# Seven block products in place of eight for two pairs of row tiles, with the weight differences on GpSimd

## The chip, the cores and the metric

The kernel runs on one core of a Trainium2 chip. The metric is the device time of one execution in microseconds. The median of three runs of the kernel before is 498.72 us (497.08 to 500.88).

## What is computed

Two layers in a row, over x of 2 x 1024 rows by 2048 columns. The first normalizes x, quantizes it and a context matrix to 8 bits, multiplies them and adds the product, times a gate, to x. The second normalizes the result, quantizes each row by its own largest value, multiplies by a weight that is rounded to -1, 0 or 1, and adds that product, times a gate, to its input. Cut to what matters:

```python
def _L0_xattn_ref(x1, x2, x1_scale, x1_zp, x2_scale, x2_zp):
    q1 = fake_quant(x1, x1_scale, x1_zp)      # clip(round(x / s + z), 0, 255), then (q - z) * s
    q2 = fake_quant(x2, x2_scale, x2_zp)
    return jnp.matmul(q1, q2)

def _L0_ffn_ref(x, weight):
    s = QP / jnp.clip(jnp.max(jnp.abs(x), axis=-1, keepdims=True), 1e-05, None)
    xq = jnp.clip(jnp.round(x * s), QN, QP) / s
    scale_w = 1.0 / jnp.clip(jnp.mean(jnp.abs(weight)), EPS, None)
    tw = jnp.clip(jnp.round(weight * scale_w), -1.0, 1.0)
    return jnp.einsum('bsi,oi->bso', xq, tw) / scale_w

x = x + jnp.tanh(g_xattn[0]) * _L0_xattn_ref(_layernorm(x), ctx_4096, ...)
x = x + jnp.tanh(g_ffn[0]) * _L0_ffn_ref(_layernorm(x), L0_ffn_weight)
```

x is (2, 1024, 2048), the context (2, 2048, 2048), the weight (2048, 2048).

## The kernel before

**Tiles.** Rows are cut into 16 tiles of 128: tiles 0 to 7 are the first batch, 8 to 15 the second. A tile of x (f32, 128 x 2048) stays in SBUF as `resid` from its load to its store. The second batch goes through in the order `rows` = 14, 15, 8, 9, 10, 11, 12, 13. In the code's key names these are x,6, x,7, x,0 to x,5, since a tile of the second batch lies where one of the first was.

**Stages of a tile.** `norm1` (statistics, L378; quantization on ScalarE, ACT, L434; clip on VectorE, DVE, L437), then a transpose by DMA into one of five `turned` buffers. `first(t, h)` multiplies it with half h of the context (1024 columns) in eight steps of four matmuls (L611) and adds the result to `resid` on DVE (L620). `column_term` sums the context's columns with PE (L581, evicted by DVE, L586), and `terms` adds these sums to a tile (L640: two SBUF tensors in, 128 x 2048). `norm2` takes the mean (L668), squares on ACT (L677), the largest square on DVE (L684), then for a group of two tiles together: `var` (L690 to L693), a square root on ACT (L697), `scale` with `newton` (L360, L366 to L368, L703, L704) and `product_scale` (L708, L709). `norm2_tile` quantizes on ACT (L748), casts on DVE (L757) and transposes by DMA (L774). `second(t, h)` multiplies with half h of the ternary weight: two units of 16 matmuls (L814), one for each quarter of 512 output columns; then an add on DVE (L823) and a store (L829), issued by GpSimd (POOL), and for the last two tiles by SyncE (SP).

**Memory.** `ca` holds the quantized context of the running batch, in 16 slots ("ca", 0) to ("ca", 15), eight for each half of the columns; slot p of half h is read by step p of every `first(t, h)`. `tw` holds the weight as fp8. PSUM has three buffers `mm` of 128 x 1024 f32, that `first` and `second` take in turn and the adds on DVE give back, and two small ones `tr`.

**The order of the work** is not left to the engines. Every piece is a step of a `Plan` with an engine, a length, a due time and what it reads and writes. `order` lays the steps out by due time as their inputs and buffers come free; `latest` works backwards from the end for new due times; ten rounds of this are made and the best order is given out. So each engine has one fixed list and takes it in order. Steps with `port=True` are planned so that DVE and POOL do not run them at once; on the chip nothing but their data holds them apart.

Of the kernel before, what the change touches and what calls it, by code (L numbers as in the profile page):

```python
# [9 lines left out]
F32 = mybir.dt.float32  # L10
# [13 lines left out]
class Plan:  # L24
# [128 lines left out]
    def give_out(self):  # L153
        steps = self.steps
        waits = [len(s[4]) for s in steps]
        follow = [[] for _ in steps]
        for n, s in enumerate(steps):
            for m in s[4]:
                follow[m].append(n)
        due, best = [s[2] for s in steps], None  # L160
        for i in range(self.ROUNDS):
            order, ends, passed = self.order(due, follow, waits)
            if best is None or max(ends) < best[0]:
                best = (max(ends), order)
            due = self.latest(ends, passed, follow)
        for n, slot in best[1]:
            if slot is None:
                steps[n][3]()
            else:
                steps[n][3](slot)  # L170
# [3 lines left out]
def flamingo_gated_kernel(  # L174
# [117 lines left out]
    plan = Plan({"work": NWORK, "tp": NTP, "mm": 3, "tr": 2})  # L292
    step = plan.step
    aT, qT, pm = {}, {}, {}
    taken = {}

    def scalars():

        s = {}

        def spread(slot):
            s["pp"] = tr[slot]
            nc.tensor.matmul(s["pp"][:, 2:6], ones32[0:1, :], par1[:, 2:6], start=True, stop=True)
            nc.tensor.matmul(s["pp"][:, 0:2], ones32[0:1, :], tg1, start=True, stop=True)

        def of(i, rs, zc):
            nc.vector.reciprocal(rs, par[:, i : i + 1])  # L310
            nc.vector.tensor_scalar(zc, par[:, i + 1 : i + 2], CENTER, None, ALU.subtract)

        def rest():
            nc.vector.scalar_tensor_tensor(g1, par[:, 2:3], par[:, 4:5], tg[:, 0:1], ALU.mult, ALU.mult)
            nc.vector.scalar_tensor_tensor(g1d1, zc1, -1.0, g1, ALU.mult, ALU.mult)
            nc.vector.scalar_tensor_tensor(g1d2, zc2, -1.0, g1, ALU.mult, ALU.mult)
            nc.vector.tensor_scalar(kd2, zc2, -float(K), None, ALU.mult)
            nc.vector.tensor_scalar(gkd, kd2, g1d1, None, ALU.mult)

        step("ACT", 0.3, 0.0, lambda: nc.scalar.activation(tg1, par1[:, 0:2], AF.Tanh), wr=[("tg1",)], hold=4.0)  # L320
        by = step("PE", 0.6, 6.0, spread, rd=[("tg1",)], wr=[("pp",)], take="tr", hold=6.8)
        step(
            "DVE", 0.2, 6.0, lambda: nc.vector.tensor_copy(par, s["pp"][:, 0:6]), rd=[("pp",)],
            wr=[("par",)], give=[by],
        )
        step("DVE", 0.3, 6.1, lambda: of(2, rs1, zc1), rd=[("par",)], wr=[("p1",)])
        step("DVE", 0.3, 6.2, lambda: of(4, rs2, zc2), rd=[("par",)], wr=[("p2",)])
        step("DVE", 0.9, 10.0, rest, rd=[("p1",), ("p2",)], wr=[("g",)])

    def res(t):  # L330
        return resid[:, t % MT, :]

    def xk(t, h=None):
        return [("x", t % MT, i) for i in ((0, 1) if h is None else (h,))]

    strip = const.tile([P, 30 * 2 * MT], F32, name="strip")
    stats6 = const.tile([P, 4, K // 512, nc.vector.BN_STATS_DIM], F32, name="stats6")
    used = [0]

    def tiny(n=1):  # L340
        used[0] += n
        return strip[:, used[0] - n : used[0]]


    def load_x(t, due, queue, halves=1, hold=0.0):
        w = K // halves
        for h in range(halves):

            def bring(h=h):
                q = nc.sync if queue == "SP" else nc.gpsimd  # L350
                q.dma_start(out=res(t)[:, ts(h, w)], in_=xrow[t][:, ts(h, w)])

            keys = xk(t) if halves == 1 else xk(t, h)
            step(queue, 0.5, due, bring, wr=keys, dma=2.55 / halves, hold=hold)

    def newton(v, sd):

        n = v.shape[1]
        r, f = tiny(n), tiny(n)
        nc.vector.reciprocal(r, sd)  # L360
        if n == 1:
            nc.vector.tensor_scalar(f, v, r, r, ALU.mult, ALU.mult)
            nc.vector.tensor_scalar(f, f, -0.5, 1.5, ALU.mult, ALU.add)
            nc.vector.tensor_scalar(r, r, f, None, ALU.mult)
        else:
            nc.vector.scalar_tensor_tensor(f, r, -0.5, r, ALU.mult, ALU.mult)  # L366
            nc.vector.tensor_mul(f, f, v)
            nc.vector.scalar_tensor_tensor(r, f, 1.5, r, ALU.add, ALU.mult)  # L368
        return r

    def norm1(group, dues, by_pe, fold_it, place=None, pieces=1, on_dve=False):

        n = len(group)
        s = {"mv": tiny(2 * n)}
        key = lambda *a: ("n1", group[0]) + a

        def stats(t, c):
            nc.vector.bn_stats(stats6[:, t % 4, c, :], res(t)[:, ts(c, 512)])  # L378

        def aggr(j, t):  # L380
            nc.vector.bn_aggr(s["mv"][:, ts(j, 2)], stats6[:, t % 4].rearrange("p c s -> p (c s)"))

        def root():
            s["sd"] = tiny(n)
            nc.scalar.activation(s["sd"], s["ve"], AF.Sqrt)

        def var():
            mv = s["mv"].rearrange("p (n s) -> p s n", s=2)
            s["mean"], s["ve"] = mv[:, 0, :], tiny(n)
            nc.vector.tensor_scalar(s["ve"], mv[:, 1, :], LN_EPS, None, ALU.add)  # L390

        def scale():
            r = newton(s["ve"], s["sd"])
            sc, bi = s["sc"], s["bi"] = tiny(n), tiny(n)
            nc.vector.tensor_scalar(sc, r, rs1, None, ALU.mult)
            if n == 1:
                nc.vector.tensor_scalar(bi, s["mean"], sc, -1.0, ALU.mult, ALU.mult)
            else:
                nc.vector.scalar_tensor_tensor(bi, s["mean"], -1.0, sc, ALU.mult, ALU.mult)
            nc.vector.tensor_scalar(bi, bi, zc1, None, ALU.add)  # L400

        for j, t in enumerate(group):
            for c in range(4):
                step(
                    "DVE", 0.69, dues[j], (lambda t, c: lambda: stats(t, c))(t, c), rd=xk(t, c // 2),
                    wr=[("st", t % 4)],
                )
            step(
                "DVE", 0.3, dues[j], (lambda j, t: lambda: aggr(j, t))(j, t), rd=[("st", t % 4)],
                wr=[key("mv")],  # L410
            )
        due = dues[-1]
        step("DVE", 0.16, due, var, rd=[key("mv")], wr=[key("ve")])
        step("ACT", 0.2, due, root, rd=[key("ve")], wr=[key("sd")])
# [4 lines left out]

    def norm1_tile(t, due, by_pe, fold_it, place, pieces, ready, scales, on_dve):  # L420

        s = {}
        key = lambda *a: ("n1t", t) + a
        n = K // pieces

# [699 lines left out]
```

## Time and profile before

| what | value |
|---|---|
| median of three runs | 498.72 us |
| the profiled execution: its time | 496.74 us |
| the profiled execution: its span | 495.0 us |
| `first`, L611, matmuls in the trace, spaced 0.216 us | 1024 |
| `second`, L814, 512-column matmuls in the trace | 976 |
| POOL's 24 TENSOR_TENSOR of 128x512 f16 (L460, L462) | 1.15 to 2.13 us each, 15 to 88 us |
| DVE L557, two SBUF tensors, 128x2048 f16, before 90 us | 1.22 to 2.17 us |
| the same after 240 us | 1.22 us |
| DVE L640, two SBUF tensors, 128x2048 f32 | 2.34 us |
| DVE L823, one PSUM and one SBUF tensor, 128x1024 f32 | 1.28 us |
| granted PE clock over the span | 0.995 |

The span is cut into stages by what PE does: up to 170 us it waits at times for data, context and weight (the two layers of the first batch meet there); from 170 us to the end it works without a gap. From 342 to 373 us PE runs `first` of the second batch, from 373 to 428 `second` of the second batch with a last tile's `first` among it, from 428 to 491 `second` alone. A line of the timeline gives start and length in us, engine, line, operation, out<-in, shape and count, and in brackets the engine's idle time before it and what ended that. A matmul's own length (379 ns) is longer than its distance to the next one (216 ns), since they are pipelined.

### The profile page before, as it was taken

The page shows a single profiled execution, that of the slowest core. Times are in us where ns is not written, and L with a number is a line of the kernel's source. Part 1 is how long each engine was busy: PE and PEld are TensorE (multiplying, and loading weights), DVE is VectorE, ACT ScalarE, POOL GpSimd, SP SyncE. Part 2 cuts the span into 40 slices and gives each one's busy share as a digit, 9 for nine tenths or more (in the row PEclk, how much of TensorE's full clock was granted, in tenths as well). Part 3 has the DMA queues.
Part 4 walks back from the last instruction along what each step waited for, and adds up shares of the span by engine and source line. Part 5 has one row for each costly group of instructions (what it writes and reads, how often), then busy time and mean ns, then how long its engine had stood idle before and what let it go on. Part 6 is the DMA issues. An engine that isn't in the chain of part 4 may idle for free.

```text
span 495.0 us, 6179 instructions
## 1 busy us (share of the span) xinstructions
PE 467.6 (94%) x2422; PEld 223.0 (45%) x2422; DVE 340.6 (69%) x568; ACT 276.6 (56%) x258; POOL 63.5 (13%) x76
## 2 busy tenths in 40 slices
PE   0599999999998799999999999999999999999996
PEld 0244454444467344444444444444444444444442
DVE  4999989959999688556697957632989831572122
ACT  4997896878999988631488364530454430050000
POOL 0574529100000020100100100000000000000000
PEclk9999999999999899999999999999999999999999
DMA  8999968992189999999999995610041542215122
GB/s 293 425 419 424 366 214 338 428 407 81 60 215 366 260 301 295 306 258 330 402 363 341 297 269 189 100 28 1 0 66 47 144 111 102 86 61 153 79 92 85
DMA packets 76170, 108.94 MB, mean 220 GB/s; under 512 B 58220, under 2 KB 58220, under 8 KB 70892
## 3 DMA queue, kind: packets, MB, share of 16 engines
q1 hardware_dynamic: 72064, 93.86, 60.1%
q0 software_dynamic: 4064, 14.68, 7.7%
q8 instruction: 19, 0.31, 0.2%
q14 instruction: 11, 0.09, 0.1%
q10 hardware_dynamic: 12, 0.00, 0.0%
HBM read 77.59 MB, written 16.78 MB: 191 GB/s over the span
## 4 chain that ended last, share of the span: by engine, by line
PE 76%; DVE 14%; DMA 6%; issue 2%; ACT 1%; DVEq 0%
PE mm L814 40%; PE mm L611 32%; DVE resid L640 3%; DMA resid<-in_x_dram 2%; PE tr L814 2%; DVE strip L684 2%; DMA tw<-in_ctx_dram 2%; DVE resid L620 2%; DMA tw<-ca 2%; DVE stats L378 1%; DVE ca L550 1%; DVE ca L903 1%; ACT ca L547 1%; PE tr L444 1%; DVE colg L557 1%
## 5 line engine op out<-in xcount | busy, mean ns | idle before, releaser
L814 PE MATMUL mm<-tw,turned 128*128 128x512 fp8e4 (+1 forms) x1104 | 211.9, 353 | 4.7 <-DMA turned<-work 2.4
L611 PE MATMUL mm<-ca,turned 128*128 128x512 f16 x832 | 187.7, 384 | 0.5 <-DVE ca L550 0.3
L814 PEld LDWEIGHTS <-turned 128*128 128x128 f16 x1168 | 106.8, 98 | 122.7 <-issue 6.3
L611 PEld LDWEIGHTS <-turned 128*128 128x128 f16 x832 | 81.8, 99 | 99.0 <-issue 4.8
L823 DVE SCALAR_TENSOR_TENSOR resid<-mm,am,resid 128x1024 f32<-128x1024 f32 (+1 forms) x31 | 38.6, 1246 | 64.3 <-PE mm L814 64.2
L547 ACT ACTIVATE ca<-ca,scal 128x2048 int16<-128x2048 f32 (+1 forms) x30 | 50.5, 1692 | 36.9 <-DMA ca<-in_ctx_dram 36.4
L677 ACT ACTIVATE work<-resid,strip 128x1024 f32<-128x1024 f32 x32 | 36.4, 1138 | 57.8 <-DVE strip L668 54.1
L829 POOL DMA_DIRECT2D out_dram<-resid x30 | 18.1, 606 | 362.5 <-DVE resid L823 225.2
L620 DVE SCALAR_TENSOR_TENSOR resid<-mm,scal,resid 128x1024 f32<-128x1024 f32 x32 | 40.4, 1277 | 18.4 <-PE mm L611 18.2
L378 DVE BATCH_NORM_STATS2 stats<-resid 128x6 f32<-128x512 f32 x64 | 40.0, 678 | 7.9 <-DMA resid<-in_x_dram 7.9
L550 DVE TENSOR_SCALAR ca<-ca 128x2048 f16<-128x2048 int16 (+1 forms) x40 | 27.3, 698 | 24.5 <-ACT ca L547 24.5
L611 PE MATMUL mm<-ca,tw 128*128 128x512 f16 x192 | 43.1, 379 | 0.4 <-DVE tw L450 0.2
L748 ACT ACTIVATE work<-resid,strip 128x2048 int16<-128x2048 f32 x16 | 35.5, 2263 | 12.2 <-DVE strip L704 7.8
L684 DVE TENSOR_REDUCE strip<-work 128x1 f32<-128x1024 f32 x32 | 37.3, 1210 | 1.3 <-ACT work L677 1.3
L640 DVE SCALAR_TENSOR_TENSOR resid<-colg,rowg,resid 128x2048 f32<-128x2048 f32 x16 | 37.4, 2344 | 0.1
L434 ACT ACTIVATE work<-resid,strip 128x2048 int16<-128x2048 f32 (+1 forms) x17 | 33.4, 1984 | 1.3 <-DVE strip L400 1.3
L557 DVE TENSOR_TENSOR colg<-colg,ca 128x2048 f16<-128x2048 f16 x24 | 30.8, 1304 | 0.3
L611 PEld LDWEIGHTS <-tw 128*128 128x128 f16 x192 | 18.4, 98 | 22.8 <-DVE tw L450 0.7
L899 ACT ACTIVATE work<-ca,scal 128x2048 int16<-128x2048 f32 x13 | 25.6, 2005 | 1.6 <-DMA ca<-in_L_ffn_weight_dram 1.1
L473 ACT ACTIVATE work<-work,scal 128x2048 f16<-128x2048 f16 x8 | 16.0, 1994 | 18.5 <-DMA turned<-work 18.5
L865 ACT ACTIVATE tw<-ca 128x2048 int8<-128x2048 f32 x10 | 19.1, 1910 | 7.6 <-DMA ca<-in_L_ffn_weight_dram 7.5
L462 POOL TENSOR_TENSOR tw<-tw,work 128x512 f16<-128x512 f16 x16 | 21.8, 1364 | 1.6 <-DVE work L437 0.4
(93 smaller groups left out, 260.7 us busy)
## 6 DMA issues: line engine op xcount, KB each, us to landing
ca<-in_L_ffn_weight_dram SPq DMA_DIRECT2D x19, 1024.0 KB, 8.6
ca<-in_ctx_dram SPq DMA_DIRECT2D x16, 1024.0 KB, 12.3
resid<-in_x_dram SPq DMA_DIRECT2D x15, 1024.0 KB, 11.7
out_dram<-resid POOLq DMA_DIRECT2D x26, 512.0 KB, 3.8
tw<-in_ctx_dram SPq DMA_DIRECT2D x8, 1024.0 KB, 12.6
ca<-in_ctx_dram SPq DMA_DIRECT2D x14, 512.0 KB, 8.4
tw<-in_L_ffn_weight_dram SPq DMA_DIRECT2D x6, 1024.0 KB, 6.8
out_dram<-resid SPq DMA_DIRECT2D x3, 512.0 KB, 2.6
```

The source lines that it names most:

```text
L378: nc.vector.bn_stats(stats6[:, t % 4, c, :], res(t)[:, ts(c, 512)])
L434: nc.scalar.activation(d, v, AF.Identity, bias=bi, scale=sc)
L547: nc.scalar.activation(a.bitcast(I16), s["w"], AF.Identity, bias=zc2, scale=rs2)
L557: nc.vector.tensor_add(r, r, a2(kt - kt % 2, h * H, 2 * H))
L611: nc.tensor.matmul(pm[t][:, ts(q, U)], aT[t][:, kt, :], a2(kt, h * H + q * U, U), start=(kt == 0), stop=(kt == KT - 1),)
L620: nc.vector.scalar_tensor_tensor(v, pm[t], g1, v, ALU.mult, ALU.add)
L640: nc.vector.scalar_tensor_tensor(v, colg, rowg[:, t : t + 1], v, ALU.add, ALU.add, accum_out=acc[:, i : i + 1])
L677: nc.scalar.activation(s["dev", t, h], res(t)[:, ts(h, H)], AF.Square, bias=s["nm"][:, j : j + 1], accum_out=s["s2"][:, k : k + 1],)
L684: nc.vector.tensor_reduce(s["m2"][:, k : k + 1], s["dev", t, h], AX.X, ALU.max)
L748: nc.scalar.activation(s["q"].bitcast(I16).rearrange("p (k j c) -> p k j c", j=2, c=P), v.rearrange("p (k c j) -> p k j c", j=2, c=P), AF. ...
L814: nc.tensor.matmul(pm[t][:, o + b0 * P : o + b1 * P], qT[t][:, k, j, :], w8[:, k, j, b0 * P : b1 * P], start=(k + j == 0), stop=(k + j == PB),
L823: nc.vector.scalar_tensor_tensor(v, pm[t][:, 0 : n * U], am[:, t : t + 1], v, ALU.mult, ALU.add)
```

## The change

For the last two pairs of tiles of the second batch, (10, 11) and (12, 13), the second product is made from seven block products in place of eight. The pair's rows, the inner dimension and the output columns are each halved; the seven products use sums of blocks of the pair (S, three new and one written over a block of tile 11 or 13) and differences of blocks of the weight (T). The differences hold integers that fp8 represents exactly. T, in eight parts of 128 x 4096 fp8, is written where half 0 of the context was (`ca` slots 0 to 7), in 64 subtractions of 128 x 512 on POOL; S is written to slots 8 to 11 by DVE. A product accumulates onto a PSUM buffer that has been read before by an add, so that one buffer serves several outputs in turn. Before, the two tiles of a pair were independent.

Beside this: the first halves of tiles 12 and 13 are both multiplied before their second halves, so that half 0 of the context comes free earlier; `norm2` of tiles 8 to 13 is done for each tile alone, with forms that have one tensor input (the pair 14, 15 keeps the form for two); `terms` of the second batch counts as `port=True` for the planner; and the plan is built twice. The first time it is the kernel before; the due times that this gives to the steps up to the second batch's `first` are kept for the second plan.

The whole body moved into a function `build(SEVEN)`, so that all lines are indented anew. The diff without that, cut to its core:

```diff
+    def rounds(self, kept=()):
...
-        due, best = [s[2] for s in steps], None
+        due, best = list(kept) + [s[2] for s in steps[len(kept) :]], None
         for i in range(self.ROUNDS):
             order, ends, passed = self.order(due, follow, waits)
             if best is None or max(ends) < best[0]:
-                best = (max(ends), order)
-            due = self.latest(ends, passed, follow)
+                best = (max(ends), due, order)
+            due = list(kept) + self.latest(ends, passed, follow)[len(kept) :]
+        return best[1:]
...
-            wr=xk(t) + [("acc", i)],
+                wr=xk(t) + [("acc", i)], port=SEVEN > 0 and t >= MT,
...
+            def var_alone():
+                vm = s["vm"] = tiny(2)
+                s2, m2, ve, big, least = s["s2"], s["m2"], vm[:, 0:1], vm[:, 1:2], tiny()
+                nc.vector.tensor_scalar(ve, s2[:, 0:1], s2[:, 1:2], None, ALU.add)
+                nc.vector.tensor_scalar(ve, ve, 1.0 / N, LN_EPS, ALU.mult, ALU.add)
+                nc.vector.tensor_scalar(big, m2[:, 0:1], m2[:, 1:2], None, ALU.max)
+                nc.vector.tensor_scalar(least, ve, Q_EPS * Q_EPS, None, ALU.mult)
+                nc.vector.tensor_scalar(big, big, least, None, ALU.max)
+            def scale_alone():
+                r = s["r"] = [newton(s["vm"][:, i : i + 1], s["sd"][:, i : i + 1]) for i in range(2)]
+                f, bi = s["f"], s["bi"] = tiny(), tiny()
+                nc.vector.tensor_scalar(f, r[1], 127.0, None, ALU.mult)
+                nc.vector.tensor_scalar(bi, s["nm"], f, None, ALU.mult)
+            def product_scale_alone():
+                a, r = am[:, group[0] : group[0] + 1], s["r"]
+                nc.vector.tensor_scalar(a, r[0], cw, r[1], ALU.mult, ALU.mult)
+                nc.vector.tensor_scalar(a, a, s["vm"][:, 1:2], None, ALU.mult)
...
+        def weight_differences(dues, engines):
+            for i, (due, by) in enumerate(zip(dues, engines)):
+                for q in range(2):
+                    b11, b12, b21, b22 = w_part(q, 0), w_part(q + 2, 0), w_part(q, 1), w_part(q + 2, 1)
+                    pair = ((b12, b11), (b22, t_part(0, q)), (b22, b12), (b21, t_part(1, q)))[i]
...
+                    for c in range(PIECES[by]):
+                        def go(i=i, q=q, by=by, pair=pair, at=ts(c, w)):
+                            eng = nc.vector if by == "DVE" else nc.gpsimd
+                            eng.tensor_tensor(
+                                t_part(i, q)[:, at], pair[0][:, at], pair[1][:, at], ALU.subtract, saturate=False
+                            )
...
+        PIECES = {"DVE": 4, "POOL": 8}
+        ENGINES = ("POOL",) * 4
+        def seven(pair, i, due, last):
+            t, u = pair
...
+            def sums(n):
+                if n == 0:
+                    nc.vector.tensor_add(s1, flat[u][:, 0:half], a22())
+                elif n == 1:
+                    nc.vector.tensor_sub(s2, s1, a11())
+                elif n == 2:
+                    nc.vector.tensor_sub(flat[u][:, 0:half], a11(), flat[u][:, 0:half])
+                else:
+                    nc.vector.tensor_sub(s4, a12(), s2)
...
+            def mult(y, a, b, q, start, slot=None):
...
+                for k in range(HK):
+                    for j in range(2):
+                        nc.tensor.matmul(
+                            s[y][:, ts(q, U)], a[:, k, j, :], moving(b(q))[:, k, j, :],
+                            start=start and k + j == 0, stop=k + j == HK, skip_group_check=not start,
+                        )
...
+            product("y", a11, lambda q: w_part(q, 0), lambda q: qt + W4(q, 0), due, start=True)
+            take("y", t, 0, due + d)
+            product("x", a12, lambda q: w_part(q, 1), lambda q: qt + W4(q, 0), due + d, start=True)
+            store(t, 0, take("x", t, 0, due + 2 * d, give=True), due + 2 * d)
+            product("y", lambda: s2, lambda q: t_part(1, q), lambda q: [keys[1]] + tk(1)(q), due + 2 * d)
+            take("y", t, 1, due + 3 * d)
+            product("z", lambda: s1, lambda q: t_part(0, q), lambda q: [keys[0]] + tk(0)(q), due + 3 * d, start=True)
+            take("z", u, 1, due + 4 * d)
+            product(
+                "y", lambda: flat[u][:, 0:half], lambda q: t_part(2, q), lambda q: [keys[2]] + tk(2)(q), due + 4 * d,
+            )
+            store(u, 1, take("y", u, 1, due + 5 * d), due + 5 * d)
+            product("z", lambda: s4, lambda q: w_part(q + 2, 1), lambda q: [keys[3]] + W4(q, 1), due + 5 * d)
+            store(t, 1, take("z", t, 1, due + 6 * d, give=True), due + 6 * d)
...
+                    "y", a22, lambda q: t_part(3, q), lambda q: qu + tk(3)(q), due + 6 * d, qs=(q,), give=give,
...
+        order = [(t, h) for h in range(2) for t in rows[:4]]
+        order += [(t, h) for t in rows[4:6] for h in range(2)]
+        order += [(t, h) for h in range(2) for t in rows[6:]]
...
+            if n == 5:
+                norm2(rows[:2], [due - 16.0, due - 8.0], False)
+            if n == 7:
+                alone(rows[2:4], due)
+        weight_differences([due + 20.0, due + 30.0, due + 40.0, due + 50.0], ENGINES)
...
-    plan.give_out()
+    plan, before = build(0)
+    due = plan.rounds()[0][:before]
+    plan, _ = build(2)
+    plan.give_out(plan.rounds(due)[1])
```

`alone` calls `norm2` for one tile at a time. `take` is the add of a product to `resid`, 128 x 1024 f32 as in `second`. In a product, "y", "x" and "z" name PSUM buffers; each product is two halves of eight matmuls.

In the program that results, the engines' lists are as they were up to the first batch's end, with few steps exchanged after it. On PE, all groups of `first` come before the first unit of `second`; behind the last column sums stand 44 groups of four matmuls (25 of them up to the end of tile 13's first half), 16 units and 28 half products. On DVE, behind the second set of column sums, stand: L640 of 14 and 15, their maxima with the add of tile 11's first half among them, the pair's `var`, the add of tile 12's first half, the pair's `scale` and `product_scale`, L640 of tile 8, the casts of 14 and 15 with L640 of tile 9 behind them, and the add of tile 13's first half. On POOL, 30 of the 64 differences come before the first store of the second batch, the rest among its stores.

## The prediction

> **What bounds the kernel now.** I read the page first, then the chain of waits, then windows of the last third, then the timeline of VectorE (DVE) and GpSimd (POOL). The page gives the span and the shares:
>
> ```profile
> span 495.0 us, 6179 instructions
> PE 467.6 (94%) x2422; PEld 223.0 (45%) x2422; DVE 340.6 (69%) x568; ACT 276.6 (56%) x258; POOL 63.5 (13%) x76
> POOL 0574529100000020100100100000000000000000
> ```
>
> TensorE (PE) is busy 94% of the span, and POOL computes nothing after 90 us. The chain of waits (start, length, what) says what sets the end:
>
> ```profile
> 342.96 30.22 PE mm L611 x140
> 373.18 17.27 PE mm L814 x80
> ...
> 428.43 62.17 PE mm L814 x288
> 490.60 0.03 issue
> 490.63 0.75 DVE resid L823
> ```
>
> From 198 us on the chain is PE alone until that last add. 62.17/288 gives 0.216 us per 512-column matmul, 0.863 per group of four. The windows (busy PE, weight loads, DVE, ACT, POOL; then PE clock, DMA) show who is nearly as full:
>
> ```profile
> 355.00:373.00 18.00, 18.00 (x85) 8.13 (x83) 16.51 (x29) 8.61 (x10) 0.00 (x0) 1.00 0.37 59
> 428.00:491.00 63.00, 62.59 (x290) 28.18 (x288) 22.98 (x33) 9.26 (x11) 3.19 (x6) 1.00 0.27 96
> ```
>
> After 428 DVE has room; from 355 to 373 it is busy 16.5 of 18 us, and the change sets POOL to work just there.
>
> **What is removed.** A pair of row tiles costs 2 x 4 x 16 = 128 matmuls in `second` and 7 x 2 x 8 = 112 in `seven`. Two pairs save 32 x 0.216 = 6.9 us of PE, all on the path; the moving operand stays fp8 of 512 columns. The last add is again of 512 columns with the same store behind it: tail 0.
>
> **PE in its new order.** All of `first` now ends before the first `second`. One group of four has moved behind the last column sums, which ended at 342.80 and so end at 341.93. Behind them stand 44 groups (38.0 us, to 379.9), 16 units of 3.45 and 28 half products of 1.73: the end is 483.5, if nothing is late.
>
> **What is added.** *DVE at the end.* 8 sums of 128x1024 f16 at half of L557's 1.22 us, 5 us, and 14 adds for 8, 6 x 1.2 = 7 us: most after 430, where DVE has 40 us free, so 0. A buffer is read by an add and then accumulated on, with one half product (1.73) between. The last matmul's own end (0.16: it lasts 379 ns at 216 spacing), the waits (0.05 and 0.06) and the add (1.28) make 1.55. It fits by 0.2; else some six places lose 0.2 each: 0 to 1.2, I take 0.
>
> *Single tiles.* Six tiles get 17 small DVE instructions each for 12 per pair: 66 more at 0.2 us, 13 us. Nearest to PE is tile 8: in front of its cast stand, from 366.4 on (below), one add, four maxima, two var, L640 and two scale, then two adds that wait for PE's 379.9, then about 7 us: cast about 390, transpose landed 5.4 later, needed six units behind 379.9, at 400.6. So 0, with 5 us of cover; past that each us is a us of PE. Three more square roots are 0.6 us of ACT, idle half the time: 0.
>
> *Queues.* SP issues the same transposes and stores; one load of x and context pieces, and the transposes of tiles 12 and 13, change places, where PE waits for none: 0. On POOL 12 stores (0.53 us each) stand among the differences; those rows are not reloaded, so a late store costs nothing, but a store that waits for an add holds the differences behind it (second rival).
>
> *64 differences on POOL.* No row shows one on fp8. Nearest is L462, two SBUF inputs, 128x512 f16: 1.15 us undisturbed, 0.08 apart, so 1.24. The range takes 1.15 (half the bytes) to 1.5. The Trainium skill, "GPSIMD Engine Reference", section "Elementwise — side-by-side cycle accounting", measures about 2.6 cycles an element at 1.2 GHz for a two-input instruction and advises VectorE for it: an estimate of 1.11 us for 512 elements, whatever their bytes, which no fp8 run here shows. They may start when the last `first` of half 0 has read its first slot, ten groups behind the sums: 350.6, say 350.8.
>
> **The wait that is added: POOL and DVE take turns.** They computed side by side in the first 90 us only:
>
> ```profile
> 15.23 1.15 POOL L460 TENSOR_TENSOR tw<-work 128x512 f16<-128x512 f16 x1 [13.92 <-DVE work L437]
> 15.42 1.24 DVE L437 TENSOR_SCALAR work<-work 128x1024 f16<-128x1024 int16 x1
> 17.38 0.27 DVE L362 TENSOR_SCALAR strip<-strip 128x1 f32<-128x1 f32 x1
> 79.17 3.54 DVE L557 TENSOR_TENSOR colg<-colg,ca 128x2048 f16<-128x2048 f16 x2
> 79.50 2.13 POOL L460 TENSOR_TENSOR tw<-work 128x512 f16<-128x512 f16 x1
> ```
>
> The clip at 15.42 takes 0.41 alone; here it ends 0.28 after POOL does. Two L557 take 3.54 where two alone take 2.45, and POOL's 1.15 became 2.13: whole instructions alternate. L362, small, one tensor input, kept its 0.27 beside POOL; L620, with one input from PSUM, its 1.28. Blocked, then, are instructions with two SBUF tensors, and f16 clips and casts. Which of these follow 350.8? The pair 14, 15 does this, in the trace with POOL idle:
>
> ```profile
> 356.23 0.15 DVE L690 TENSOR_TENSOR strip<-strip 128x2 f32<-128x2 f32 x1
> ...
> 356.49 0.15 DVE L692 TENSOR_TENSOR strip<-strip 128x2 f32<-128x2 f32 x1
> 356.68 0.16 DVE L693 SCALAR_TENSOR_TENSOR strip<-strip 128x2 f32<-128x2 f32 x1
> ```
>
> and L366, L367, L368, L704, L708, L709 after them: nine tiny instructions with two SBUF tensors. This pair keeps its form; only later tiles get forms with one tensor input. None of the nine ever ran beside POOL. By size the nearest row is L362 (no wait), by operation and operands L557 (up to a whole wait). I go by operands, as the large L620 did not wait either: size is not what decides. The Trainium skill, "SBUF — State Buffer", section "Who interferes with whom", says that a DVE instruction with two SBUF inputs contends with a GpSimd instruction that reads SBUF, and that the second fully blocks; L557 agrees, no run here shows a tiny one; by this rule the sum is the one below, and without it the gain of 6.9 would stand.
>
> *What stands behind them on DVE:* L690 to L693, the add of tile 12's first half, newton to L704, L708 and L709, L640 of tile 8, casts of 14 and 15, L640 of tile 9, then the add of tile 13's first half, which frees the PSUM buffer for its second half. Undisturbed: sums evicted by 344.0, two L640 and means to 348.8, four L684 and one add to 354.7; then 0.53, 1.2, 1.1, 0.33, 2.35, 0.6, 2.0 (the second cast, behind ACT's 2.26 us quantization), 2.35, 1.2: done 366.4. PE wants the buffer 30 groups behind the sums, at 341.93 + 25.9 = 367.8. Slack 1.4 us.
>
> With POOL always ready, thirteen instructions there take turns (nine tiny, two L640, two casts). A wait is half a piece (0.58) at random, a whole one (1.15) right behind another such instruction: 7.5 to 15 us. I take 0.7 each, 9.1, nearer the half, since some fall behind the add or ACT and a waiting instruction has its fixed part behind it (the clip's 0.28 for 0.41). Less the slack, PE stands 7.7 us (6.1 to 13.6). And its clock falls after idling:
>
> ```profile
> 169.31 12.21 PE L814 MATMUL mm<-tw,turned 128*128 128x512 fp8e4 x48 [2.33 <-DMA tw<-ca]
> 170.00:173.00 3.00, 3.00 (x9) 0.53 1.06 299
> ```
>
> After 2.33 us idle the granted clock was 0.53 for a while; 48 matmuls took 12.21 for 10.36: 1.85 us more. Sum: -6.9 + 7.7 + 1.85 = +2.7 us (+1.0 to +8.6). The profiled run took 496.74 (1.7 beside its span), so 499.4 there; the median is 498.72, 2.0 above it, so I predict 501.4.
>
> **Rivals.** *Faster: the tiny ones do not wait.* Then two L640 and two casts are left, 4 x 0.58 = 2.3 at random, of which ACT's gap of 1.4 and the slack of 1.4 take all: -6.9, 491.8. For it: L362, and that no tiny one was ever seen to wait. Against: their operands.
>
> *Slower: the differences come late.* The fourth difference is needed behind 16 units and 13 half products: 379.9 + 55.2 + 22.4 = 457.5 for its first half, 461.0 for its second. From 350.8 on POOL yields the port to DVE for 24 us (six L640 14, eight casts 5.5, four sums 2.6, the nine 1.5) and spends 5 on stores, so (457.5 - 350.8 - 29)/61 leaves 1.27 us for each of the 61 pieces up to there, against 1.24. PE's own delay of 9.6 moves this to 1.43. At 1.5, 350.8 + 96 + 29 = 475.8 against 461.0, and 1.85 of clock: -6.9 + 14.8 + 1.85 = +9.7, 508.4. For it: no fp8 row, stores that wait for adds, and that POOL's 24 large pieces took from 15 to 88 us before. Against: L462's 1.15. It decides from 1.3 us a piece without the first stall, from 1.45 with it.
>
> *It does not do what it says:* the number of matmuls is in the program, so this lies only in their speed. Stationary f16 from another tile, moving fp8 with the same step of 2: I give it nothing.
>
> **How the numbers follow.** Forecast 0.58, faster rival 0.23, slower rival 0.19. About 1% (5 us, 493.7 to 503.7) is what a measurement of this kernel can tell. Of the forecast's +1.0 to +8.6 a quarter of the chance lies above +5: 0.14 slower, 0.44 same. The faster rival is all faster, 0.23. The slower one is 0.17 slower, 0.02 same. Range: the faster rival must be in (491.8, less 0.4 for a shorter tail), and above the forecast's likely part to +7: 491.4 to 505.7. The forecast's own range is 499.7 to 507.3.
>
> **What would show it.** Matmuls 32 fewer, at 0.216. After the column sums a PE gap of 6 to 14 us, 30 groups on, released by a DVE add (resid), a clock near 0.5 behind it, and L692, L693, L367, L368 at about 1 us in place of 0.16: right. If these stay at 0.16 and PE has no gap after 350: the faster rival. Pieces of 1.5 us or more, and a gap in the products released by POOL: the slower one. Wrong altogether would be a gap that starts in a transpose of tile 8 or in the bank reads of `seven`.

## The result and the profile after

| | before | after |
|---|---|---|
| time, median (lowest to highest), us | 499.8 (497.1 to 505.6), 4 runs | 518.3 (517.3 to 519.5), 4 runs |
| ratio, 95% interval | | 1.039 (1.033 to 1.045) |
| profiled run / its span, us | 496.74 / 495.0 | 518.92 / 517.2 |
| PE busy, us (matmuls recorded) | 467.6 (2422) | 467.0 (2390) |
| DVE busy / POOL busy, us | 340.6 / 63.5 | 401.3 / 138.2 |

The kernel became 3.9% slower; 501.4 us was predicted, with a range that ended at 505.7. Ratios, here and below, leave out executions that were over 1.5% slower than their kernel's fastest; medians and ranges are of all runs. The shares and three rows of slices from the page of the kernel after:

```profile
span 517.2 us, 6289 instructions
PE 467.0 (90%) x2390; PEld 220.0 (43%) x2390; DVE 401.3 (78%) x648; ACT 277.9 (54%) x261; POOL 138.2 (27%) x140
...
PE   0589999999987999999979999999859999795996
POOL 0565637000000110001001000005996256266000
PEclk9999999999999899999989999999979999887999
```

PE has the 32 matmuls less, but its row has holes where before there were none, in slices 21, 29, 30, 35 and 37, and POOL is at work beside all but the first. The waits of PE (in total, how many, longest; us) name who ended each hole:

```profile
PE mm L625 <- DVE resid L634: 8.6, 1, 8.6
...
PE mm L975 <- DVE resid L998: 5.3, 1, 5.3
PE mm L625 <- DMA turned<-work: 3.2, 1, 3.2
PE mm L855 <- DVE resid L864: 3.1, 1, 3.1
```

The timeline of PE gives their places, and the slow clock behind them (start, length, what):

```profile
268.23 5.95 PE L625 MATMUL mm<-ca,turned 128*128 128x512 f16 x20 [3.21 <-DMA turned<-work]
...
381.24 13.52 PE L625 MATMUL mm<-ca,turned 128*128 128x512 f16 x56 [8.64 <-DVE resid L634]
...
449.69 9.94 PE L855 MATMUL mm<-tw,turned 128*128 128x512 fp8e4 x32 [3.12 <-DVE resid L864]
...
475.25 3.57 PE L975 MATMUL mm<-ca,turned 128*128 128x512 fp8e4 x8 [5.26 <-DVE resid L998]
478.62 2.30 PE L975 MATMUL mm<-tw,ca 128*128 128x512 fp8e4 x8
```

At the spacing that this view shows elsewhere (0.216 us, the full clock), 56 matmuls take 12.26 us, 32 take 7.07, 8 take 1.89 and 20 take 4.49. So the balance reads: -6.9 for the 32 matmuls; +17.0 for three gaps behind DVE (8.64, 3.12, 5.26) and +6.2 for the clock behind them (1.26, 2.87, 2.09); +4.7 for the gap at 265 us with its clock (3.21 and 1.46); +0.8 for a longer tail (the last matmul ends 5.2 us before the end, 4.4 before). That is +21.8 of the 22.2 us by which the span grew.

What DVE did ahead of the three gaps stands in its timeline; the predicted one first:

```profile
359.13 1.03 DVE L726 TENSOR_SCALAR strip<-strip 128x2 f32<-128x2 f32 x1
360.07 1.13 DVE L727 TENSOR_TENSOR strip<-strip 128x2 f32<-128x2 f32 x1
...
370.62 3.26 DVE L654 SCALAR_TENSOR_TENSOR resid<-colg,rowg,resid 128x2048 f32<-128x2048 f32 x1
373.81 0.08 DVE L654 DVE_READ_ACCUMULATOR resid<-colg,rowg,resid 128x1 f32 x1
373.81 1.57 DVE L797 CAST work<-work 128x2048 f16<-128x2048 int16 x1
...
416.32 5.08 DVE L797 CAST work<-work 128x2048 f16<-128x2048 int16 x1
...
433.80 9.59 DVE L797 CAST work<-work 128x2048 f16<-128x2048 int16 x1
...
461.47 12.54 DVE L959 TENSOR_TENSOR ca<-turned,ca 128x1024 f16<-128x1024 f16 x1
```

The small instructions take 1.0 us in place of 0.15, as forecast: each waits for one piece. The last three lines were not forecast. A cast takes 0.68 us alone, and the fourth sum (L959) too; here they take 5.1, 9.6 and 12.5. POOL's timeline shows for what:

```profile
413.43 7.41 POOL L931 TENSOR_TENSOR ca<-tw 128x512 fp8e4<-128x512 fp8e4 x7
431.69 1.63 POOL L870 DMA_DIRECT2D out_dram<-resid  x3 [10.85 <-DVE strip L374]
433.33 5.30 POOL L931 TENSOR_TENSOR ca<-tw 128x512 fp8e4<-128x512 fp8e4 x5
...
441.76 1.08 POOL L931 TENSOR_TENSOR ca<-tw 128x512 fp8e4<-128x512 fp8e4 x1
...
461.25 0.58 POOL L870 DMA_DIRECT2D out_dram<-resid  x1 [4.50 <-DVE resid L864]
461.85 11.61 POOL L931 TENSOR_TENSOR ca<-tw,ca 128x512 fp8e4<-128x512 fp8e4 x11
```

The runs of pieces end at 420.84, 442.84 and 473.46, and the three DVE instructions 0.56, 0.55 and 0.55 us later. They did not get in after one piece, but only when the whole run was over; below, this is called starving. L959 had even begun before its run, at 461.47, while GpSimd was issuing a store (461.25 to 461.83). Behind the cast at 433.80 stand an addition of the column term, the maxima and the add that frees a PSUM buffer (the gap at 446); behind L959 stands the add of the bank read (the gap at 470).

### The profile page after: what moved, and what is told of

Its sections match the earlier page's. It is cut to its first block, busy times and chain, and to the rows that moved or that the text cites. A ratio compares the mean times of both kernels' runs of the same rounds, so it can differ in the third digit from the quotient of the medians.

```text
span 517.2 us, 6289 instructions
## 1 busy us (share of the span) xinstructions
PE 467.0 (90%) x2390; PEld 220.0 (43%) x2390; DVE 401.3 (78%) x648; ACT 277.9 (54%) x261; POOL 138.2 (27%) x140
## 4 chain that ended last, share of the span: by engine, by line
PE 56%; DVE 29%; DMA 8%; issue 5%; ACT 1%; SPq 1%; DVEq 0%; ACTq 0%
PE mm L625 28%; PE mm L855 18%; PE mm L975 7%; DVE resid L654 6%; DMA resid<-in_x_dram 5%; DVE strip L698 4%; DVE work L797 4%; DVE resid L634 2%; PE tr L855 2%; DMA turned<-work 2%; DVE ca L564 2%; DMA tw<-ca 2%; DVE resid L864 1%; DVE ca L1102 1%; ACT work L691 1%
## 5 line engine op out<-in xcount | busy, mean ns | idle before, releaser
L855 PE MATMUL mm<-tw,turned 128*128 128x512 fp8e4 (+1 forms) x848 | 158.8, 349 | 8.1 <-DVE resid L864 3.1
L625 PEld LDWEIGHTS <-turned 128*128 128x128 f16 x832 | 81.7, 99 | 114.5 <-issue 16.8
L855 PEld LDWEIGHTS <-turned 128*128 128x128 f16 x912 | 82.3, 99 | 98.5 <-issue 14.3
L870 POOL DMA_DIRECT2D out_dram<-resid x26 | 16.0, 617 | 221.5 <-DVE resid L864 180.7
L634 DVE SCALAR_TENSOR_TENSOR resid<-mm,scal,resid 128x1024 f32<-128x1024 f32 x32 | 40.5, 1278 | 26.9 <-PE mm L625 26.7
L931 POOL TENSOR_TENSOR ca<-tw 128x512 fp8e4<-128x512 fp8e4 x32 | 34.5, 1104 | 74.0 <-PE mm L625 74.0
L564 DVE TENSOR_SCALAR ca<-ca 128x2048 f16<-128x2048 int16 (+1 forms) x40 | 27.1, 697 | 22.2 <-ACT ca L561 21.9
L931 POOL TENSOR_TENSOR ca<-tw,ca 128x512 fp8e4<-128x512 fp8e4 x32 | 40.6, 1297 | 0.0
L654 DVE SCALAR_TENSOR_TENSOR resid<-colg,rowg,resid 128x2048 f32<-128x2048 f32 x16 | 39.8, 2495 | 0.1
L864 DVE SCALAR_TENSOR_TENSOR resid<-mm,am,resid 128x1024 f32<-128x1024 f32 x22 | 28.1, 1277 | 10.7 <-PE mm L855 10.7
L998 DVE SCALAR_TENSOR_TENSOR resid<-mm,am,resid 128x1024 f32<-128x1024 f32 (+1 forms) x15 | 18.0, 1208 | 19.8 <-PE mm L975 19.8
```

The costliest lines, as they stand in the source:

```text
L564: nc.vector.tensor_scalar(a, a.bitcast(I16), -128.0, 127.0, ALU.max, ALU.min)
L625: nc.tensor.matmul(pm[t][:, ts(q, U)], aT[t][:, kt, :], a2(kt, h * H + q * U, U), start=(kt == 0), stop=(kt == KT - 1),)
L634: nc.vector.scalar_tensor_tensor(v, pm[t], g1, v, ALU.mult, ALU.add)
L654: nc.vector.scalar_tensor_tensor(v, colg, rowg[:, t : t + 1], v, ALU.add, ALU.add, accum_out=acc[:, i : i + 1])
L855: nc.tensor.matmul(pm[t][:, o + b0 * P : o + b1 * P], qT[t][:, k, j, :], w8[:, k, j, b0 * P : b1 * P], start=(k + j == 0), stop=(k + j == PB),
L931: eng.tensor_tensor(t_part(i, q)[:, at], pair[0][:, at], pair[1][:, at], ALU.subtract, saturate=False)
```

## The experiments

Line numbers in the lines below are those of each run's own kernel; an edit that adds lines moves the numbers behind it.

**No pieces.** Is it GpSimd, or the instructions that DVE got in addition?

```diff
-                            eng.tensor_tensor(
-                                t_part(i, q)[:, at], pair[0][:, at], pair[1][:, at], ALU.subtract, saturate=False
-                            )
+                            pass
```

> GpSimd issues none of the 64 differences (four of the seven products of each pair then multiply by what the context's buffers held before, so rows of these two pairs are not the reference's); every other instruction stands where it stood. Theory P (DVE waits for GpSimd's pieces): the tiny instructions of pair 14, 15 go back to 0.15 us, the casts and the fourth sum to 0.7, the three gaps of 8.6, 3.1 and 5.3 us and the slow clock behind two of them go, about 20 us; only the early gap of 3.2 us and its clock are left: 498 us (496 to 500). Rival L (DVE's own added work: six tiles normalised one by one, eight sums, fourteen adds): with GpSimd idle DVE has the same list, so the gaps stay by more than half: over 508 us.

Measured: 495.9 us (493.1 to 501.5, 10 runs), 0.996 (0.992 to 1.000) of before. From its timeline of DVE, the cast and the fourth sum that starved:

```profile
427.32 0.68 DVE L797 CAST work<-work 128x2048 f16<-128x2048 int16 x1
...
449.60 0.69 DVE L956 TENSOR_TENSOR ca<-turned,ca 128x1024 f16<-128x1024 f16 x1
```

All three gaps behind DVE are gone; the one at 265 us stays (4.8 us). The single-tile forms, the sums and the adds of `seven` therefore cost PE nothing where no pieces run beside them; the pieces do the harm, some 22 us of it.

**Early list, and the kernel before again.** Did PE's new order make the gap at 265 us?

```diff
+    moved = [s for s in order if 793 <= s[0] <= 796]
+    order = [s for s in order if s not in moved]
+    i = [n for n, _ in order].index(804) + 1
+    plan.give_out(order[:i] + moved + order[i:])
```

> In the list of PE alone, the first four groups of tile 14 move behind the next unit of tile 4 and two more groups of tile 15, so that PE asks for tile 14's transpose 4.3 us later; no other instruction moves. Theory O (the new order of the list made the early gap): the 3.2 us gap at 265 us goes, with the 0.9 clock behind it, and the sums end at about 342 in place of 346.5; the pieces then start 4.6 us earlier too, and the later gaps keep their size: 513.5 us (512 to 515). Rival J (the transposes ran late for another reason, a jitter of the DMA): the gap comes back elsewhere or was not in most runs: 517 to 519 us.

> The kernel before, unchanged, with its waits once more. Theory T (the transposes of the second batch land at the edge of what PE's list allows, before and after): a wait of PE for a transpose or a context piece of 0 to 3 us shows between 255 and 300 us, beside 0 in the first profile. Theory O (the new list of the kernel after makes it): none again, as in the first profile.

Measured: 515.8 us (513.2 to 518.1), and before once more 505.2 us in one run. Their timelines of PE:

```profile
289.00 46.75 PE L625 MATMUL mm<-ca,turned 128*128 128x512 f16 x208 [3.93 <-DMA turned<-work]
```

```profile
267.52 4.45 PE L611 MATMUL mm<-ca,turned 128*128 128x512 f16 x12 [3.07 <-DVE stats L378]
```

The gap left 265 us and came back at 285, behind the next transpose. And the kernel before, which had none there in its first profile, has one of 3.07 us in its second, which is a single run and names another releaser (DVE's statistics, not the transpose). So a gap can open in this stretch in both kernels; the profiles of the other variants have 0.4 to 4.8 us there. Whether the change makes it larger isn't shown either way; the 4.7 us stay out of what the change is charged with.

**Small instructions in one-tensor forms.** The pair 14, 15 gets the forms of `alone`, column by column, for instance:

```diff
+                if group[0] == ONE:
...
+                    for j in range(n):
+                        c = slice(j, j + 1)
+                        nc.vector.tensor_scalar(ve[:, c], s2[:, c], s2[:, n + j : n + j + 1], None, ALU.add)
...
                 nc.vector.tensor_add(ve, s2[:, 0:n], s2[:, n : 2 * n])
```

> The nine tiny instructions of pair 14, 15 with two tensors become sixteen with one tensor and a scalar from a column, in the same steps. If the operands decide (the prediction's step): each takes 0.2 us beside a piece, the nine save about 9 x 1.03 and cost 18 x 0.2, so DVE gains 5 to 6 us there and the gap of 8.6 us at 372.6 shrinks to 2 to 4 us; the two later gaps may change places but not go: 511 us (508 to 514). Rival (any DVE instruction waits for a piece, or the two additions of the column term and the casts make the gap): the new ones take 0.6 to 1 us each and the time is 518 or more.

Measured: 517.0 us (511.7 to 519.6). From its timelines of DVE and PE:

```profile
361.02 0.20 DVE L739 TENSOR_SCALAR strip<-strip 128x1 f32<-128x1 f32 x1
...
361.51 0.95 DVE L741 TENSOR_SCALAR strip<-strip 128x2 f32<-128x2 f32 x1
362.49 1.02 DVE L742 TENSOR_SCALAR strip<-strip 128x2 f32<-128x2 f32 x1
```

```profile
379.33 14.68 PE L635 MATMUL mm<-ca,turned 128*128 128x512 f16 x56 [4.43 <-DVE resid L644]
```

The first gap halves (8.64 to 4.43), the other two are as before (3.12 and 5.26). Forms of one column pass at 0.2 us. But L741 and L742 have one tensor and still wait: for TENSOR_SCALAR two columns are enough. So the number of tensors isn't the whole rule, and the columns aren't either: in the same stretch a RECIPROCAL of 128x4 with one tensor (L376) took 0.17. The time, for which 508 to 514 was expected, fell by less than the runs scatter.

**Casts and sums of every second element.** Is it the fast form of a copy that starves?

```diff
-                nc.vector.tensor_copy(s["q"], s["q"].bitcast(I16))
+                even = lambda v: v.rearrange("p (c j) -> p j c", j=2)
+                nc.vector.tensor_copy(even(s["q"]), even(s["q"].bitcast(I16)))
```

> The casts of the eight tiles of the second batch and the eight sums read and write every second element, in two halves (the same values). Theory F (only the fast form of a DVE copy or f16 sum, two or four elements a cycle, waits until GpSimd's whole run of pieces is over): in this form the casts take about 2.2 us beside pieces or without them, in place of 5.1, 9.6 and 12.5, the fourth sum about 2.2; the gaps of 3.1 and 5.3 us go, the gap of 8.6 stays or grows by the casts' 1.5 us: 510 us (507 to 514). Rival (the order of issue or the length of the run decides, not the form): these instructions still take 5 us and more somewhere, and the time is 518 or more.

Measured: 517.9 us (515.6 to 519.8). From its timeline of DVE:

```profile
419.87 5.75 DVE L801 CAST work<-work 128x2048 f16<-128x2048 int16 x1
...
438.65 10.29 DVE L801 CAST work<-work 128x2048 f16<-128x2048 int16 x1
...
467.22 1.31 DVE L964 TENSOR_TENSOR ca<-turned,ca 128x1024 f16<-128x1024 f16 x1
...
471.53 2.31 DVE L801 CAST work<-work 128x2048 f16<-128x2048 int16 x1
```

This form of the cast takes 1.37 us alone and starved twice all the same, so my theory F fell. The gap that stood at 446 grew to 5.7 us. But the one that stood at 470 went (0.7 us is left): the fourth sum (L964) did not wait, and a cast behind it waited for one piece. Their run of pieces, from 466.94 on, began right behind a store too; a DVE instruction was in progress when it began, and GpSimd took 14.14 us for the 11 pieces, 11.61 in the kernel after.

**The port by itself.** Three runs put pieces of GpSimd and single DVE instructions beside each other, without PE.

> Not the kernel's work: eleven runs of GpSimd pieces (128x512, two SBUF inputs), each with a few DVE instructions that begin behind the first piece; the output is one row of zeros. It tells apart what decides whether a DVE instruction beside a run gets in after one piece or only behind the whole run. Theory F (form): a 128x2048 f16 cast waits for the whole run in A, B, I and J, the f32 addition of two tensors (B, K) for at most one piece. Theory H (history): the cast waits for the whole run in A (nothing before it), but for one piece only in B, where the f32 addition has just made GpSimd wait. Theory G (gap): the pieces of A overlap by 0.05 us and never leave the port; with a gap (C: each piece reads the one before; D: a memset between; F: f16 pieces) the cast gets in after one piece. E: of the small ones, those of two columns with one tensor take 0.9 to 1.0 us, those of one column 0.2 whatever the number of tensors, if the fast form decides; if two tensors decide, the additions of one column take 1.0 us and the two-column one with one tensor 0.2.

> Not the kernel's work: runs of GpSimd pieces with a cast or an addition of DVE in the middle, as before; what differs is what GpSimd issued ahead of the run and when DVE arrives. In the kernel all three starved instructions stood beside runs that GpSimd began right after issuing a store; the casts that waited for one piece stood beside the run that began with no store. Theory S (a store issued ahead makes GpSimd keep the port through the run): casts wait 0.9 to 1.1 us in A, B, C, L and for the whole rest of the run (9 us and more) in D and E; a memset behind the store (F) or between the pieces (G) or a large addition ahead (H) may end it. Theory Y (the moment of arrival decides): B and C differ from A, D does as A. Theory Z (f16 pieces, 1.00 us apart, leave no gap): J and K starve, whatever was before, and this says nothing of fp8.

> Not the kernel's work: more runs of pieces with one cast, with another moment of arrival in each (0 to 11 us behind the first piece) with and without a store ahead; one with an addition early and 8 us without a request; one behind large reductions; a store that is followed by a wait of GpSimd for DVE before the run; a store and a transpose issued by SyncE beside the run. Theory S (a store of GpSimd's own, until it next stops): starves in all runs with the store except the two in which GpSimd waits for DVE behind it; nowhere else. Theory Y (phase): both kinds mixed, with and without stores. Theory D (a DMA in flight, whoever issued it): the two with SyncE starve as well, which would also cover the cast of 26.7 us beside SyncE's transposes.

From the first one, DVE: a cast beside ten fp8 pieces; then small instructions; then a cast beside ten f16 pieces.

```profile
25.43 1.49 DVE L52 CAST q<-q 128x2048 f16<-128x2048 int16 x1
...
79.62 0.20 DVE L91 TENSOR_SCALAR s<-s 128x1 f32<-128x1 f32 x1
79.75 0.84 DVE L92 TENSOR_TENSOR s<-s 128x1 f32<-128x1 f32 x1
...
81.56 1.14 DVE L94 TENSOR_SCALAR s<-s 128x2 f32<-128x2 f32 x1
...
96.52 9.42 DVE L52 CAST q<-q 128x2048 f16<-128x2048 int16 x1
```

One tensor and one column: free. Two tensors, or a TENSOR_SCALAR of two columns: a piece. And the same cast waits for one piece or for the rest of the run. In the second one, with a store issued by GpSimd just ahead, a cast, and later the large f32 addition of two tensors, starve:

```profile
70.88 11.99 DVE L53 CAST q<-q 128x2048 f16<-128x2048 int16 x1
...
130.31 15.70 DVE L55 SCALAR_TENSOR_TENSOR v<-u,s,v 128x2048 f32<-128x2048 f32 x1
```

The tally of the three: behind a store of GpSimd's own, DVE waited for the whole rest of the run in 12 of 12 stretches (memsets of one column between the pieces didn't help), and for one piece in the one stretch where GpSimd had stood 2.2 us waiting for DVE after the store. (In the other stretch meant so, DVE was done before, and GpSimd did not stop; it starved.) Without such a store DVE starved in 5 of 28, at no moment of arrival that I could make a rule of. All five are among the 19 runs of pieces that GpSimd began without standing idle before; of the nine that it began after waiting for DVE, none starved. That would fit the mending below, but the counts are small. So the form, the moment and the gap between pieces don't decide by themselves. A store ahead was enough in every stretch of these benches, but it is not needed, and in the kernels it was not always enough: the fourth sum of the variant above did not wait behind one, and in turns, below, a sum behind two stores (L963, 1.47 us) waited for one piece.

**Stores on another queue.** If a store ahead is what does it in the kernel, SyncE's queue should mend it.

```diff
-                q = nc.sync if t in final else nc.gpsimd
+                q = nc.sync if t >= MT else nc.gpsimd
...
-                    e = nc.sync if r in final else nc.gpsimd
+                    e = nc.sync
```

> All stores of the second batch are issued by SyncE in place of GpSimd, at the same places of the plan; no other instruction is changed. Theory S (stores make GpSimd keep the port): no cast or sum waits longer than about 1.6 us, the gaps of 3.1 and 5.3 us go, the first gap of 8.6 stays: 509 us (506 to 512). The differences also end some 30 us earlier, since GpSimd waits for no add. Rival Q (the length of an unbroken run decides): the run is now longer still, 40 pieces and more, a cast in it starves for 10 us and more, and the time is 518 or above.

Measured: 528.0 us (527.1 to 533.3). Its timelines of DVE and PE:

```profile
401.88 26.71 DVE L797 CAST work<-work 128x2048 f16<-128x2048 int16 x1
```

```profile
432.11 33.88 PE L855 MATMUL mm<-tw,turned 128*128 128x512 fp8e4 x144 [21.20 <-DVE strip L682]
```

The stores had also broken up the runs, since GpSimd waits there for adds. Without them the pieces run on, and one cast starved for 26 us: rival Q. Where DVE starves, what is left of the unbroken run is the price, whatever sets the kind of waiting.

**Turns.** Then runs must end where DVE is due. The plan knows the order of casts and pieces; the program did not enforce it. One column copied by GpSimd behind each such DVE step does:

```diff
+        def turn_over(v):
+            nc.gpsimd.tensor_copy(turn1, v)
...
                 nc.vector.tensor_copy(s["q"], s["q"].bitcast(I16))
+                if t >= MT:
+                    turn_over(s["q"][:, 0:1])
```

and the same behind L654 (its accumulated column) and the first pair's last sum. Two variants add an edit from above.

> Behind each addition of the column terms, each cast of the second batch and the last sum of the first pair, GpSimd copies one column of what DVE has just written: so the pieces that the plan puts behind that DVE step now wait for it, and DVE meets at most the pieces planned before it. If the loss is the waiting of DVE behind pieces (whatever makes it long or short): no cast or sum waits longer than the pieces planned ahead of it, the small instructions of pair 14, 15 meet six pieces in place of twenty, the gap of 8.6 us falls to under 4, those of 3.1 and 5.3 go: 503 us (499 to 508). Rival R (GpSimd has too little time for 64 pieces if it yields): the last difference ends after 480 us, PE waits for it, 510 us or more.

> The same, and the nine small instructions of pair 14, 15 in forms with one tensor, column by column. If both causes add: 2 to 4 us less than with the turns alone, 500 us (497 to 505). If the turns alone have freed that stretch: no difference.

> The turns, and the stores of the second batch issued by SyncE in place of GpSimd. If a cast starves because pieces run on unbroken, the 26.7 us of the run with SyncE's stores and its gap of 21.2 us go: from 528 to 503 us (498 to 508). If SyncE's stores themselves hold back the transposes: PE waits for a transpose late in the second products, 510 us or more.

| | us, median (range) | ratio to before, 95% interval |
|---|---|---|
| turns | 495.2 (492.0 to 500.3), 10 runs | 0.996 (0.992 to 0.999) |
| turns, one-tensor forms | 498.5 (494.1 to 501.8), 10 runs | 0.999 (0.995 to 1.003) |
| turns, stores by SyncE | 496.0 (490.6 to 501.1), 10 runs | 0.993 (0.989 to 0.997) |

From turns, POOL stops after six pieces until DVE's addition is done, and DVE's next steps run as if alone:

```profile
355.83 6.36 POOL L939 TENSOR_TENSOR ca<-tw 128x512 fp8e4<-128x512 fp8e4 x6 [1.61 <-PE mm L626]
367.21 0.51 POOL L668 COPY turn<-acc 128x1 f32<-128x1 f32 x1 [5.03 <-DVE resid L655]
```

```profile
364.11 0.17 DVE L744 TENSOR_SCALAR strip<-strip 128x2 f32<-128x2 f32 x1
...
364.72 2.35 DVE L655 SCALAR_TENSOR_TENSOR resid<-colg,rowg,resid 128x2048 f32<-128x2048 f32 x1
...
446.23 3.09 DVE L967 TENSOR_TENSOR ca<-turned,ca 128x1024 f16<-128x1024 f16 x1
```

The fourth sum waits 2.4 us, for two pieces that the plan puts ahead of it, and from 250 us on no gap of PE behind DVE is longer than 0.3 us. From the variant with SyncE's stores, PE's timeline after the sums:

```profile
342.27 38.19 PE L626 MATMUL mm<-ca,turned 128*128 128x512 f16 x176
380.30 48.51 PE L863 MATMUL mm<-tw,turned 128*128 128x512 fp8e4 x224
```

PE runs through; its last matmul ends at 484.1, where the prediction's count gave 483.5, and the span is 489.5 us, 5.5 below the first profile of before. GpSimd had time enough (rival R fell): its last piece ended at 460 us in turns. The one-tensor forms add nothing that can be measured once the turns are there. Against the kernel before, turns and turns with SyncE's stores are ahead by 0.4 and 0.7% by their ratios, and by 2.1 and 1.3 us by the medians (497.3 for before). That is little, less than the runs of one kernel scatter.

## Why the prediction was wrong

- **-6.9 us of PE:** right. 2390 recorded matmuls for 2422, at the same spacing, and no wait in the half products other than the one named below. In the time less of it shows: turns and turns with SyncE's stores are about 2 and 3.4 us below before, by their ratios, and the profile of turns has a gap of 3.5 us at 265 us.
- **PE's new order:** right. The prediction had the 44 groups end at 379.9; in turns with SyncE's stores, whose gap at 265 us was only 0.5 us, they end at 380.3. In the kernel after everything from 268 us on is 4.6 us late by that gap, which the forecast didn't have and the kernel before shows too at times.
- **The first wait:** right in place and releaser, and in size partly by luck: 30 groups behind the sums, behind the add of tile 13's first half, 8.64 us for 7.7 (6.1 to 13.6). The terms inside were off and made up for each other. Eleven small instructions waited, not nine: nine by about 0.9, L380 by 0.6, L725 by 0.2. With two L654 and two casts, 0.8 to 0.9 each, that is 12.3 us for the 9.1 forecast, and slack and ACT's gap took more of it. L726 and L738 have one tensor, but two columns. "I go by operands" was thus only half of the rule: in the bench and in tiny_one, forms of two columns with one tensor waited too. The clock behind this gap cost 1.26 us for 1.85.
- **The skill's rule** (the Trainium skill, "SBUF — State Buffer", "Who interferes with whom"): two SBUF inputs, or a mode of DVE that uses both ports, and the second to issue blocks until the first is done. The small instructions agree (0.20 us with one column of one tensor, 0.84 with two tensors, 1.14 with two columns). What it says of blocking for the length of the other instruction does not always hold here: beside the waits of one piece stand instructions of 5.1 to 26.7 us against pieces of 1.05 us, and L959, which had begun before the first piece of its run, waited for all of them.
- **64 pieces at 1.24 us:** too dear. Fp8 pieces come 1.05 us apart (14 in 14.79). The slower rival, differences that come late, is out: no gap of PE was released by POOL. It had the right direction, by the wrong mechanism.
- **"most after 430, where DVE has 40 us free, so 0"**, and for the single tiles "So 0, with 5 us of cover": this is the step that failed. The prediction priced turns only up to the add of tile 13, and let a DVE instruction wait for one piece at most, from clips and L557 beside f16 pieces in the first 90 us. The casts and sums beside the later pieces got no price. They waited until the run of pieces was over: 4.4, 8.9 and 11.9 us by the lines above, in place of 0 to 1.15. Room in a stretch of 60 us says nothing for an instruction with PE's buffer a few us behind it. This cost the gaps of 3.12 and 5.26 and 4.96 of clock: 13.3 us, more than the whole miss of the range.
- **"A store that waits for an add holds the differences behind it":** it did (but for one store, POOL issued nothing from 395.6 to 410.8 us, and nothing from 420.8 to 431.7), and it was priced as lateness. What it did was to gather the pieces into runs beside the casts, each begun right behind a store. Whether the store is why DVE starved there stays open.
- **Single tiles, sums and adds by themselves:** 0 for PE, right, by no_pieces; not so beside pieces.
- **Bank read then accumulate:** it fits; the gap at 470 us is the late add behind L959, not the read itself.

## What to carry over

By these runs, a second engine that shares a port is not priced by the share of time that it takes, but by the longest run that it can do without a stop: read the list of both engines and ask of each short instruction on the path how many of the other's pieces can stand together in front of it. If a plan has them take turns, make the program take them too: copies of one column, 0.2 us each where GpSimd need not wait for DVE, turned 518 us into 495. Before an early gap is put down to a change, profile the kernel before a second time.

## What the runs showed of the hardware

- A DVE instruction that needs the shared port either gets in after the piece in progress (waits of 0.8 to 1.1 us, many times in a row; in the kernel after, GpSimd was not slowed by the small ones, 14 pieces in 14.79 us, while in tiny_one they took 17.30) or not before GpSimd stops (up to 26 us). Both were seen for the same cast. In the benches it was always the second behind a store issued by GpSimd, if GpSimd did not stop in between (12 of 12), and sometimes without one (5 of 28); in the kernels a store ahead did not always do it, and the 26.7 us came without one. What sets it stays open.
- Beside fp8 pieces, f32 TENSOR_SCALAR of 128x2 with one tensor waits as the instructions with two do (1.14 us), 128x1 with one tensor does not (0.20). A RECIPROCAL of 128x4 (0.16) and TENSOR_REDUCE of 128x1024 (three in 3.46) in the kernel after did not wait.
- Pieces of 128x512 with two inputs come 1.05 us apart in fp8; with the memset of one column between them, 1.09.
